# Scores of causal attention by 64 keys, with only the queries that may see them, and the first roots written to PSUM a step later

## Chip, cores and metric

The kernel runs on one core of a Trainium2 chip, all in fp32. The metric is device time in microseconds (us) of one execution, the median of the runs of a kernel. The core has five engines that run side by side and wait for each other by semaphores: TensorE (PE in the profile; its weight loads are shown apart as PEld), VectorE (DVE), ScalarE (ACT), GpSimd (POOL) and SyncE (SP), which issues the transfers. [...]

## What is computed

The input x has the shape (2, 256, 128, 128): batch, time, bands, channels. Three residual blocks follow each other; the first is causal attention over the 256 times of each of the 2x128 sequences, with four heads of 32 channels. The other two (attention over bands within 16 of each other, and a feed-forward block) are left out of this extract.

```python
def _mha(x, wi, bi, wo, bo, h, mask):
    qkv = x @ wi.T + bi
    q, k, v = jnp.split(qkv, 3, axis=-1)
    ...
    scores = jnp.einsum('...hqd,...hkd->...hqk', q, k) * (1.0 / np.sqrt(dh)) + mask
    attn = jax.nn.softmax(scores, axis=-1)
    o = jnp.einsum('...hqk,...hkd->...hqd', attn, v)
    o = o.swapaxes(-2, -3).reshape(x.shape)
    return o @ wo.T + bo
...
cm = _causal_mask(x.shape[1])
xt = _ln(x, ln_t_w, ln_t_b).transpose(0, 2, 1, 3)
x = x + _mha(xt, t_wi, t_bi, t_wo, t_bo, H_T, cm).transpose(0, 2, 1, 3)
```

## The kernel before

**Groups and steps.** The work is cut into groups of four tiles of 128 rows. A group of the time stage (class `OverTime`) is two sequences of 256 times, so each sequence is two tiles; there are 128 such groups. After them come the groups of the band attention (`OverBands`) and of the feed-forward block (`FeedForward`), in runs of eight. `run` (from L1029) goes through steps n and calls, by hand, the parts of several groups in each: every engine executes its instructions in exactly the order in which `run` calls them (`InOrder`), and the semaphore waits are put in by the framework from the tiles that instructions share. All instructions are recorded at one helper's line, L859, so a group of instructions is known by its tiles.

**A step of the time stage** calls, in this order: the scores (`time_scores`, L726: second key tile of group n, "old", and first key tile of group n+1, "new", interleaved in a fixed list of sixteen calls that ends with heads 1 and 2 of the second tile); the exponentials of the scores, six 128-partition instructions on ScalarE in a row (`second_weights` of heads 0 and 3, `first_weights` of heads 1 and 2, `second_weights` of heads 1 and 2); the mask of the second tile and `add(0)` on GpSimd; transfers; `statistics` of group n+5 on VectorE (four bn_stats and four bn_aggr); `normalize` and `turn` of group n+4 on VectorE (xh, and z, the 32x32 transpose, which four DMAs write to memory in a turned order, from where a later `fetch` reads xnT); `weigh` of group n-1 on TensorE (rp, the sums of the weights, and op, the weighted values); `invert` on ScalarE (ln and r, the reciprocals); the two remaining first exponentials, `mask_first` and `add(1)`; `output` of group n-2 on TensorE (yp) and `finish` on VectorE (res); `divide` of group n-1 on VectorE (rp, u, oT); queries and keys of group n+2 (qp, kp on TensorE, qT and kT on ScalarE); then the root of group n+5; `bias` on GpSimd; and the values (vp on TensorE, copied to v by ScalarE).

**The root.** `root_by_scalar` computes 1/sqrt(var + eps) roughly on ScalarE, as Exp(-0.5 Ln(var + eps)), for four columns; `refine` takes one Newton step on it with three VectorE instructions (`vy`, `vy`, `rstd`). `root0` is an SBUF tile. `normalize` of that group comes one step later.

**Scores.** A product of a head has the head's 32 channels as rows, 128 keys as the columns of the weights and the queries as the moving operand. The first key tile meets 256 queries and the second the 128 that come after it; the part above the diagonal is computed and then set to 0 by GpSimd's affine_select after the exponential. Each head has a bank of its own. TensorE works on the four heads' row groups side by side; the other products (`product`) are cut into four column groups of 32.

**Banks.** In the time stage each bank has a name, and the names turn round after each step:

```python
self.banks = dict(zip(("a1", "a2", "b0", "b3", "a0", "a3", "b1", "b2"), range(8)))
...
Attention.place = dict(rp=b["b0"], op=b["b3"], yp=b["a1"], qp=b["a2"], kp=b["b1"], vp=b["b2"])
...
self.banks = dict(
    a1=b["a1"], a2=b["a2"], b0=b["a0"], b3=b["a3"], a0=b["b0"], a3=b["b1"], b1=b["b3"], b2=b["b2"]
)
```

So `s1` of head 2 (the second tile's scores, 256 columns) and later in the step `vp` (512 columns) share bank b2; and the bank of `op`, which `divide` reads last, is the bank of head 1's second scores in the next step, that of `rp` the bank of head 0's first scores.

Of the kernel before, what the change touches and what calls it, by code (L numbers as in the profile page):

```python
# [10 lines left out]
F32 = mybir.dt.float32  # L11
# [9 lines left out]
H = 4  # L21
# [6 lines left out]
GB = 16  # L28
RUN = 32
SAFE = 30.0  # L30
LARGE = 1e20
EXP_SET = "natural_log_exp_and_others"

# [391 lines left out]
class Group:  # L425
# [30 lines left out]
        gpsimd.tensor_scalar(self.rstd, self.mv[:, :, 1], EPS, None, ALU.add)  # L456
        gpsimd.tensor_tensor(self.rstd, self.rstd, path.k.mhalf, ALU.pow)

    def root_by_scalar(self):

        path = self.path
        ln = path.small.tile([P, NT], F32, name="lnv")
        path.scalar.activation(ln, self.mv[:, :, 1], AF.Ln, bias=path.eps)
        self.root0 = path.small.tile([P, NT], F32, name="root0")
        path.scalar.activation(self.root0, ln, AF.Exp, scale=-0.5)

    def refine(self):

# [89 lines left out]

class Attention(Group):
    which = None  # L560
    place = {}

    def bias(self):
# [23 lines left out]
    def values(self):  # L587
        path = self.path
        wv = path.k.wf[self.which][:, 2 * P : 3 * P]
        self.vp = path.bank([P, NT, P], "vp", self.place.get("vp"))  # L590
        for i in range(NT):
            product(path, self.vp[:, i], self.xnT[:, i * P : (i + 1) * P], wv)

    def take_values(self):
        path = self.path
# [43 lines left out]
def rows_of(h):  # L639
    return slice(h * D, (h + 1) * D)  # L640


def product(path, out, weights, x, start=True, stop=True):


    for c in range(P // D):
        path.tensor.matmul(out[rows_of(c)], weights[:, rows_of(c)], x, start=start, stop=stop)


class OverTime(Attention):  # L650

    which = 0
    early, late = (1, 2), (0, 3)

    def first_tiles(self):
# [10 lines left out]

    def first_scores(self, h, s):
        r, a = rows_of(h), 2 * s * P  # L670
        self.path.tensor.matmul(
            self.s0[h][:, s], self.kT[r, a : a + P], self.qT[r, a : a + 2 * P], start=True, stop=True
        )

    def second_scores(self, h, s):
        r, a = rows_of(h), (2 * s + 1) * P
        self.path.tensor.matmul(
            self.s1[h][:, s], self.kT[r, a : a + P], self.qT[r, a : a + P], start=True, stop=True
        )

    def first_weights(self, heads):
        for h in heads:
# [3 lines left out]
        for h in heads:  # L686
            self.path.scalar.activation(self.p1[:, :, h, 0], self.s1[h], AF.Exp)

    def mask(self, blk):
        path = self.path  # L690
        path.gpsimd.affine_select(
            out=blk, in_=blk, compare_op=ALU.is_ge, fill=path.zero, base=0,
            pattern=[[0, 2], [0, H], [1, P]], channel_multiplier=-1,
        )

    def mask_first(self):
        self.mask(self.p0[:, :, :, 0:P])

    def mask_second(self):
        self.mask(self.p1[:, :, :, 0])  # L700

    def add(self, s):
        self.path.gpsimd.tensor_tensor(self.p1[:, s, :, 1], self.p1[:, s, :, 0], self.p0[:, s, :, P : 2 * P], ALU.add)
# [160 lines left out]
class BoundedPath:  # L864
    def __init__(self, ctx, tc, k):
        self.tc, self.nc, self.k = tc, tc.nc, k
        self.xpool = ctx.enter_context(tc.tile_pool(name="xpool", bufs=3))
        self.work = ctx.enter_context(tc.tile_pool(name="work", bufs=3))
        self.small = ctx.enter_context(tc.tile_pool(name="small", bufs=6))
        self.ps = ctx.enter_context(tc.tile_pool(name="ps", bufs=1, space=PSUM))  # L870
        self.next_bank = 0
        self.held = {}
        self.banks = dict(zip(("a1", "a2", "b0", "b3", "a0", "a3", "b1", "b2"), range(8)))
        self.tensor, self.vector = InOrder(tc, tc.nc.tensor), InOrder(tc, tc.nc.vector)
        self.scalar, self.gpsimd = InOrder(tc, tc.nc.scalar), InOrder(tc, tc.nc.gpsimd)
        self.sync = InOrder(tc, tc.nc.sync)
        self.dram = ctx.enter_context(tc.tile_pool(name="turns", bufs=3, space=DRAM))
        self.zero = 0.0
        self.once = once = ctx.enter_context(tc.tile_pool(name="once", bufs=1))
        self.eps = once.tile([P, 1], F32, name="eps")  # L880
        tc.nc.vector.memset(self.eps, EPS)

        self.band = once.tile([P, P], F32, name="band")
        tc.nc.gpsimd.memset(self.band, 0.0)
        for s in (1, -1):
            tc.nc.gpsimd.affine_select(
                out=self.band, in_=self.band, compare_op=ALU.is_ge, fill=-1e30, base=BAND,
                pattern=[[-s, P]], channel_multiplier=s,
            )
# [4 lines left out]

    def bank(self, shape, name, i=None):

        return self.ps.tile(shape, F32, name=name, tag=f"ps{self.turn_of_bank() if i is None else i}")

    @staticmethod
    def of_times(ap, i, f):  # L900
# [128 lines left out]
    def run(self, x, out):  # L1029
# [21 lines left out]
        for n in range(-12, len(groups) + 2):  # L1051
            feeds = [at(n - 2 + i, FeedForward) for i in range(5)]
            bands = [at(n - 2 + i, OverBands) for i in range(5)]
            turn = feeds[2] and bands[1]
            old, new = (groups[i] if at(i, OverTime) else None for i in (n, n + 1))
            if bands[2] and feeds[1]:
                self.scalar.preload_act_table_set(EXP_SET)
            do_at(n + 4, FeedForward, "root")
            do(n, "first_half", "first_function", "first_mask")
            if old is not None or new is not None:  # L1060
                time_scores(old, new)
                b = self.banks
                Attention.place = dict(rp=b["b0"], op=b["b3"], yp=b["a1"], qp=b["a2"], kp=b["b1"], vp=b["b2"])
            else:
                Attention.place = {}
            if old is not None:
                old.second_weights(old.late)
            if new is not None:
                new.first_weights(new.early)
            if old is not None:  # L1070
                old.second_weights(old.early)
                old.mask_second()
                old.add(0)
            if turn:
                do(n, "second_half", "second_function")
            do_at(n + 3, OverTime, "fetch")
            do_at(n + 2, (OverBands, FeedForward), "fetch")

            for i in (2 * n + 12, 2 * n + 13) if n < -2 else (n + 10,) if n < 2 else ():
                if i >= NT:  # L1080
                    do(i, "load")
            if n < -8 or n >= 0:
                do(n + 12, "load")
            if n >= 0:
                do_at(n + 5, OverTime, "statistics")
                for i in due[n]:
                    do(i, "statistics")
            do_at(n + 3, (OverBands, FeedForward), "normalize", "turn")
            do_at(n + 4, OverTime, "normalize", "turn")
            if n < 0:  # L1090
                do(n + 5, "statistics")
            do_at(n + 5, FeedForward, "statistics")
            if n == -4:
                self.fold_rest()
                self.warm()
            do(n - 1, "weigh")
            do(n - 1, "invert_exactly" if turn else "invert")
            if new is not None:
                new.first_weights(new.late)
                new.mask_first()  # L1100
            if old is not None:
                old.add(1)
            if bands[2] or turn or old is not None:
                do(n - 2, "output", "finish")
            do(n - 1, "divide")
            if not turn:
                do(n, "second_half", "second_function")
            if n in run0:
                do(n, "bias")
            if not bands[2] and old is None:  # L1110
                do_at(n, FeedForward, "bias")
                do_at(n + A, OverBands, "bias")
                if at(n - 1, FeedForward) and at(n - 2, OverBands):
                    do_at(n + A - 1, OverBands, "statistics", "root")
                if not turn:
                    do_at(n + A, OverBands, "statistics", "root")
            do_at(n + 2, OverTime, "queries_keys", "take_query", "take_key")
            do_at(n + 1, OverBands, "queries_keys", "take_query", "take_key")
            do_at(n + 5, OverTime, "root_by_scalar", "refine")
            for i in due[n]:  # L1120
                do(i, "root_by_scalar", "refine")
            do_at(n, OverTime, "bias")
            if not bands[2] and not turn and old is None:
                do(n - 2, "output", "finish")
            do_at(n + 2, OverTime, "values", "take_values")
            do_at(n + 1, OverBands, "values", "take_values")
            if old is not None or new is not None:

                b = self.banks
                self.banks = dict(  # L1130
                    a1=b["a1"], a2=b["a2"], b0=b["a0"], b3=b["a3"], a0=b["b0"], a3=b["b1"], b1=b["b3"], b2=b["b2"]
                )
# [69 lines left out]
```

## Time and profile before

| what | us |
|---|---|
| median of 3 runs | 2708.69 (2707.76 to 2710.78) |
| span of the profiled execution | 2709.9 |
| of it, up to the end of the time stage | about 957 |
| ACT, busy in the window 60 to 957 us | 789.56 |
| POOL, busy in the same window | 723.86 |

The groups of instructions in the window 100 to 900 us, which holds 110 steps of the time stage (columns: line, engine, operation, tiles, shapes, count, then busy us, mean ns of one, then idle us of the engine just before them and what ended it):

```profile
L859 PE MATMUL sp<-qT,kT 32*128 32x256 f32 x1758 | 174.2, 387 | 0.0
L859 PEld LDWEIGHTS sp<-qT,kT 32*128 32x128 f32 x3517 | 155.3, 185 | 23.0 <-ACT kT L859 21.8
L859 PE MATMUL sp<-qT,kT 32*128 32x128 f32 x1755 | 150.0, 286 | 0.0
L859 POOL TENSOR_SCALAR_AFFINE_SELECT p<-p 128x1024 f32<-128x1024 f32 x219 | 239.7, 1095 | 144.0 <-ACT p L859 144.0
L859 DVE SCALAR_TENSOR_TENSOR vy<-mv,root 128x4 f32<-128x4 f32 x110 | 115.7, 1052 | 0.0
L859 ACT ACTIVATE lnv<-mv,eps 128x4 f32<-128x4 f32 x110 | 32.9, 299 | 0.0
```

A shape such as 32*128 is the rows and columns of the weights that are in use; 32x256 is the moving operand. Matmuls overlap, so a group's busy time is less than its count times its mean. A step runs two of the GpSimd masks and one each of the last two rows. An engine's idle time matters only if what ended it lies on the chain of waits.

### The profile page before, as it was taken

The numbers are of one execution on the slowest core, as the hardware profiler recorded it, in microseconds if no ns is written. First come the engines' busy times: TensorE is split into PE (matmuls) and PEld (weight loads), VectorE is DVE, ScalarE is ACT, GpSimd is POOL, SyncE is SP. The second block draws the span as 40 slices with busy tenths as digits, with TensorE's granted clock in tenths as the row PEclk, the third lists the DMA queues.
The fourth block names the chain that finished last, engine by engine and source line by source line (L and its number), as shares of the span: only waits on it lengthen the run. The fifth ranks groups of instructions, "written<-read, shape, count | busy, mean of one in ns | idle before, by whom it ended". The sixth has DMA issues, their size and how long they took to land.

```text
span 2709.9 us, 139654 instructions
## 1 busy us (share of the span) xinstructions
PE 2677.1 (99%) x60470; PEld 1831.5 (68%) x60470; DVE 2279.5 (84%) x6708; ACT 1845.1 (68%) x3620; POOL 1864.3 (69%) x2169
## 2 busy tenths in 40 slices
PE   7999999999999999999999999999999999999998
PEld 5666676766676666666667766666666666666665
DVE  7999999999999997868769779688697796886874
ACT  5888888888888874655746646557456465565563
POOL 3788888878887876667657566666676666665762
PEclk9999999999999999999999999999999999999999
DMA  5555555555555535445444454444444444544533
GB/s 145 142 151 145 147 150 144 149 147 145 149 141 148 150 99 132 108 119 133 110 124 125 108 130 113 120 129 114 121 127 110 124 119 119 130 109 123 134 91 84
DMA packets 471442, 346.00 MB, mean 128 GB/s; under 512 B 43296, under 2 KB 405152, under 8 KB 470816
## 3 DMA queue, kind: packets, MB, share of 16 engines
q1 hardware_dynamic: 469568, 335.92, 47.8%
q8 instruction: 476, 7.80, 1.2%
q10 hardware_dynamic: 1248, 1.05, 0.2%
q14 instruction: 150, 1.23, 0.2%
HBM read 169.03 MB, written 167.77 MB: 124 GB/s over the span
## 4 chain that ended last, share of the span: by engine, by line
PE 84%; DVE 12%; DMA 2%; issue 1%; SPq 0%; ACT 0%; DVEq 0%; ACTq 0%
PE zp L859 17%; PE hp L859 14%; PE sp L859 11%; PE op L859 8%; PE rp L859 7%; PE vp L859 7%; PE qp L859 7%; PE kp L859 7%; PE yp L859 6%; DVE xh L859 2%; DVE stats L859 2%; DMA xnT<-turned 2%; DVE z L859 2%; DVE u L859 2%; DVE rp L859 1%; DVE x L859 1%
## 5 line engine op out<-in xcount | busy, mean ns | idle before, releaser
L859 ACT ACTIVATE hT<-hp,b 128x512 f32<-128x512 f32 x512 | 346.7, 687 | 533.3 <-PE hp L859 518.4
L859 POOL TENSOR_SCALAR_AFFINE_SELECT pf<-pf 128x512 f32<-128x512 f32 x768 | 476.9, 635 | 264.6 <-ACT pf L859 238.2
L859 DVE TENSOR_SCALAR xh<-x,mv,rstd 128x160 f32<-128x160 f32 x1536 | 597.5, 432 | 14.2
L859 PEld LDWEIGHTS zp<-w2T_sb,hT 128*32 128x32 f32 x16384 | 459.3, 110 | 61.5 <-issue 37.2
L859 PE MATMUL zp<-w2T_sb,hT 128*32 128x128 f32 x16384 | 475.8, 273 | 0.2 <-ACT hT L859 0.2
L859 PE MATMUL hp<-xnT,w1f 128*32 128x512 f32 x4096 | 474.6, 592 | 0.0
L859 ACT ACTIVATE p<-sp 128x512 f32<-128x512 f32 (+1 forms) x1024 | 417.1, 500 | 15.7 <-PE sp L859 4.0
L859 POOL TENSOR_SCALAR_AFFINE_SELECT p<-p 128x1024 f32<-128x1024 f32 x256 | 280.2, 1094 | 190.8 <-ACT p L859 190.8
L859 PE MATMUL sp<-qT,kT 32*128 32x128 f32 (+1 forms) x8192 | 361.2, 310 | 3.2 <-DVE oT L859 1.8
L859 PEld LDWEIGHTS sp<-qT,kT 32*128 32x128 f32 x8192 | 309.2, 185 | 56.9 <-ACT kT L859 48.0
L859 PEld LDWEIGHTS vp<-wf,xnT 128*32 128x32 f32 x8192 | 232.7, 110 | 157.3 <-issue 138.8
L859 POOL TENSOR_TENSOR p<-p,p 128x512 f32<-128x512 f32 x256 | 328.8, 1284 | 10.7
L859 DVE BATCH_NORM_STATS2 stats<-x 128x6 f32<-128x128 f32 x1536 | 327.1, 276 | 1.0 <-DMA x<-in_x 1.0
L859 ACT ACTIVATE pf<-sp 128x512 f32<-128x512 f32 x512 | 264.7, 603 | 60.4 <-PE sp L859 59.6
L859 PEld LDWEIGHTS hp<-xnT,w1f 128*32 128x32 f32 x4096 | 156.3, 110 | 190.0 <-issue 115.5
L859 DVE STREAM_TRANSPOSE z<-xh 128x512 f32<-128x512 f32 x384 | 273.3, 712 | 13.2
L859 DVE TENSOR_TENSOR res<-zp,res 128x512 f32<-128x512 f32 x128 | 87.6, 684 | 223.5 <-PE zp L859 223.5
L859 PE MATMUL yp<-wn,oT 128*32 128x128 f32 x8192 | 271.8, 273 | 0.0
L859 PE MATMUL vp<-wf,xnT 128*32 128x128 f32 x8192 | 270.9, 273 | 0.0
L859 POOL TENSOR_TENSOR rstd<-rstd,mhalf 128x4 f32<-128x4 f32 x248 | 256.6, 1035 | 20.7
L859 PE MATMUL qp<-xnT,wf 128*32 128x512 f32 x2048 | 267.2, 592 | 2.0 <-ACT p L859 2.0
L859 ACT ACTIVATE qT<-qp,bq 128x512 f32<-128x512 f32 x256 | 176.1, 688 | 134.4 <-PE qp L859 134.3
(92 smaller groups left out, 4003.1 us busy)
## 6 DMA issues: line engine op xcount, KB each, us to landing
turned<-z SPq DMA_DIRECT2D x1536, 64.0 KB, 2.2
xnT<-turned SPq DMA_DIRECT2D x384, 256.0 KB, 3.1
x<-in_x SPq DMA_DIRECT2D x128, 256.0 KB, 4.2
x<-res SPq DMA_DIRECT2D x256, 128.0 KB, 2.4
x<-x SPq DMA_DIRECT2D x128, 256.0 KB, 4.4
out<-res SPq DMA_DIRECT2D x256, 128.0 KB, 2.5
w1T_sb<-in_w1T ACTq DMA_DIRECT2D x1, 256.0 KB, 6.8
w2T_sb<-in_w2T ACTq DMA_DIRECT2D x1, 256.0 KB, 8.3
```

The source lines that it names most:

```text
L859: return self.tc.keep_in_program_order(emit(*args, **kwargs))
```

## The change

- **Scores.** A product is cut into two of 64 keys. The first key tile's upper half (keys 64 to 127) gets only the queries from 64 on; of the second tile the upper half (keys 64 to 127, with the queries from 64 on) is written to partitions 0 to 63 and the lower half (all 128 queries) to partitions 64 to 127. The columns left out are not written: what the bank held before goes through the exponential there, and the mask sets it to 0.
- **Values.** In tiles 1 and 3 (the second key tile of each sequence) `product` takes the weight columns, which are the keys, in the order 2, 3, 0, 1 (its `turn` is added to c, modulo four), so that the rows of v stand as those of the scores do.
- **Mask of the second tile.** Two affine_selects, one on partitions 0 to 63 over 128 queries, one on partitions 64 to 127 over the first 64.
- **Roots.** Groups of the time stage write `root0` to the last four columns of bank b2, in the step after; the two ScalarE instructions stand ahead of the step's exponentials, the three of `refine` between `statistics` and `normalize`. The groups of the bands keep `root_by_scalar` with an SBUF tile.
- **Banks.** Each bank is one tile for the whole run, of which `bank` returns a part, in place of a new tile at each use.

```diff
-    def root_by_scalar(self):
+    def root_by_scalar(self, to=None):
...
-        self.root0 = path.small.tile([P, NT], F32, name="root0")
+        self.root0 = path.small.tile([P, NT], F32, name="root0") if to is None else to
         path.scalar.activation(self.root0, ln, AF.Exp, scale=-0.5)
+
+    def root_in_bank(self):
+        path = self.path
+        self.root_by_scalar(path.ps[path.banks["b2"]][:, BANK - NT :])
...
-            product(path, self.vp[:, i], self.xnT[:, i * P : (i + 1) * P], wv)
+            product(path, self.vp[:, i], self.xnT[:, i * P : (i + 1) * P], wv, turn=2 if i in self.swapped else 0)
...
+    swapped = (1, 3)
...
     def first_scores(self, h, s):
         r, a = rows_of(h), 2 * s * P
-        self.path.tensor.matmul(
-            self.s0[h][:, s], self.kT[r, a : a + P], self.qT[r, a : a + 2 * P], start=True, stop=True
-        )
+        for e in range(0, P, HALF):
+            self.path.tensor.matmul(
+                self.s0[h][e : e + HALF, s, e:], self.kT[r, a + e : a + e + HALF], self.qT[r, a + e : a + 2 * P],
+                start=True, stop=True,
+            )
 
     def second_scores(self, h, s):
         r, a = rows_of(h), (2 * s + 1) * P
-        self.path.tensor.matmul(
-            self.s1[h][:, s], self.kT[r, a : a + P], self.qT[r, a : a + P], start=True, stop=True
-        )
+        for e in range(0, P, HALF):
+            q = P - HALF - e
+            self.path.tensor.matmul(
+                self.s1[h][e : e + HALF, s, q:], self.kT[r, a + q : a + q + HALF], self.qT[r, a + q : a + P],
+                start=True, stop=True,
+            )
...
     def mask_second(self):
-        self.mask(self.p1[:, :, :, 0])
+        self.mask(self.p1[0:HALF, :, :, 0], -HALF)
+        self.mask(self.p1[HALF:P, :, :, 0, 0:HALF])
...
-        self.ps = ctx.enter_context(tc.tile_pool(name="ps", bufs=1, space=PSUM))
+        ps = ctx.enter_context(tc.tile_pool(name="ps", bufs=1, space=PSUM))
+        self.ps = [ps.tile([P, BANK], F32, name=f"bank{i}", tag=f"bank{i}") for i in range(8)]
...
+            do_at(n + 4, OverTime, "root_in_bank")
             if old is not None:
                 old.second_weights(old.late)
...
-            do_at(n + 4, OverTime, "normalize", "turn")
+            do_at(n + 4, OverTime, "refine", "normalize", "turn")
...
-            do_at(n + 5, OverTime, "root_by_scalar", "refine")
```

More of the change, by code (lines that the diff above doesn't have):

```diff
@@ L30 @@
 SAFE = 30.0
+BANK = 512
+HALF = P // 2
 LARGE = 1e20
@@ L560 @@
     which = None
+    swapped = ()
     place = {}
@@ L640, in rows_of, with product @@
     return slice(h * D, (h + 1) * D)
-def product(path, out, weights, x, start=True, stop=True):
+def product(path, out, weights, x, start=True, stop=True, turn=0):
     for c in range(P // D):
-        path.tensor.matmul(out[rows_of(c)], weights[:, rows_of(c)], x, start=start, stop=stop)
+        path.tensor.matmul(out[rows_of(c)], weights[:, rows_of((c + turn) % NT)], x, start=start, stop=stop)
 class OverTime(Attention):
     which = 0
+    swapped = (1, 3)
     early, late = (1, 2), (0, 3)
@@ L687, in second_weights, with mask @@
             self.path.scalar.activation(self.p1[:, :, h, 0], self.s1[h], AF.Exp)
-    def mask(self, blk):
+    def mask(self, blk, base=0):
         path = self.path
         path.gpsimd.affine_select(
-            out=blk, in_=blk, compare_op=ALU.is_ge, fill=path.zero, base=0,
-            pattern=[[0, 2], [0, H], [1, P]], channel_multiplier=-1,
+            out=blk, in_=blk, compare_op=ALU.is_ge, fill=path.zero, base=base,
+            pattern=[[0, 2], [0, H], [1, blk.shape[-1]]], channel_multiplier=-1,
         )
@@ L895, in bank @@
     def bank(self, shape, name, i=None):
-        return self.ps.tile(shape, F32, name=name, tag=f"ps{self.turn_of_bank() if i is None else i}")
+        flat = self.ps[self.turn_of_bank() if i is None else i][:, 0 : math.prod(shape[1:])]
+        if len(shape) == 2:
+            return flat
+        names = "abc"[: len(shape) - 1]
+        sizes = dict(zip(names, shape[1:]))
+        return flat.rearrange(f"p ({' '.join(names)}) -> p {' '.join(names)}", **sizes)
     @staticmethod
```

## The prediction

> **What bounds the kernel now.** I read the page first. Its line of busy times says that TensorE hardly rests; the chain of waits puts the time stage, the only one that the change touches, at 32 to 957 us.
>
> ```profile
> PE 2677.1 (99%) x60470; PEld 1831.5 (68%) x60470; DVE 2279.5 (84%) x6708; ACT 1845.1 (68%) x3620; POOL 1864.3 (69%) x2169
> ```
>
> Then the stage by itself, in the view of windows (columns: stretch, length, busy PE, PEld, DVE, ACT, POOL, clock, DMA share, GB/s). PE is busy all of the time, but VectorE 97% of it: two engines share the lead.
>
> ```profile
> 100.00:900.00 800.00, 800.00 (x17513) 557.53 (x17507) 777.33 (x2186) 703.88 (x1642) 646.89 (x549) 1.00 0.56 147
> ```
>
> Third, the chain of waits cut to one step (start, length, what). A step is scores, sums, weighted values, output, queries, keys, values: 401.90 to 409.19 is 7.29 us, and the mean over the stage is 7.31 (every third step is some 0.06 longer). PE's own order is the whole chain.
>
> ```profile
> 401.90 1.53 PE sp L859 x24
> 403.42 1.00 PE rp L859 x16
> 404.42 1.30 PE op L859 x32
> 405.72 0.87 PE yp L859 x32
> 406.60 0.86 PE qp L859 x8
> 407.46 0.86 PE kp L859 x8
> 408.31 0.87 PE vp L859 x32
> 409.19 1.56 PE sp L859 x25
> ```
>
> Last, the timeline of the engines that feed it. The reader is to see that VectorE's oT ends at 402.65, inside PE's scores, and that the first refine line lasts 1.07 us for four columns, while GpSimd's bias runs to 403.63.
>
> ```profile
> 401.96 0.69 DVE L859 TENSOR_TENSOR oT<-op,u 128x512 f32<-128x512 f32 x1
> 402.57 1.07 DVE L859 SCALAR_TENSOR_TENSOR vy<-mv,root 128x4 f32<-128x4 f32 x1
> 403.68 0.16 DVE L859 SCALAR_TENSOR_TENSOR vy<-vy,root 128x4 f32<-128x4 f32 x1
> 403.88 0.16 DVE L859 SCALAR_TENSOR_TENSOR rstd<-vy,root 128x4 f32<-128x4 f32 x1
> 405.02 1.58 DVE L859 TENSOR_SCALAR xh<-x,mv,rstd 128x160 f32<-128x160 f32 x4
> 409.29 0.69 DVE L859 TENSOR_TENSOR oT<-op,u 128x512 f32<-128x512 f32 x1
> ```
>
> ```profile
> 401.90 0.20 ACT L859 ACTIVATE root<-lnv 128x4 f32<-128x4 f32 x1
> 402.01 0.57 ACT L859 COPY v<-vp 128x512 f32<-128x512 f32 x1
> 402.68 2.19 ACT L859 ACTIVATE p<-sp 128x256 f32<-128x256 f32 x6
> ```
>
> [...] vy with mv and root takes 1.07 us and ends with GpSimd's bias, the next two take 0.16. [...] The trace shows it only for four tiles (128x32: 32 of vp in 0.87 us, eight in a row per column group, 0.109 each).
>
> **Part 1, scores by 64 keys.** A head's scores are two instructions per product, and 128 columns of one take 0.109 us. Before, a head's row group streams 2x256 and 2x128 columns, twice: 1536 columns, 1.31 of the 1.53 us. After, each half of the row group streams 2x(256+64) or 2x(192+128) = 640, twice: 1.09 us, if the halves run side by side. That is 0.22 less; the first weight load is shorter too (185 ns for 128 columns, 110 for 32, so about 135 for 64): 0.05. Together 0.27 us a step. The other bound: halves one after the other, 2560 columns, 2.18 us, 0.87 more. I take side by side, as the column groups of vp do.
>
> **Part 2, halves exchanged.** The values' weight columns only change places: nothing. GpSimd's second mask becomes two: the 64-partition one keeps its 1024 elements per partition (1.09 us), the other has 512 (0.63 in the bands' row pf). GpSimd goes from 6.0 busy us a step to 6.6, and its chain from the last exponential to add(1) grows by 0.6.
>
> **Part 3, the roots.** Ln and Exp move, on ScalarE, from ahead of the copy of v to ahead of the six exponentials of the next step; no DMA moves, and none waits for them. The three refine instructions move on VectorE from the step's end past four statistics and four aggregates to just before normalize. [...]
>
> But the roots lie in bank b2, which also holds head 2's second scores, the last product of the scores. [...] ScalarE's Exp must wait for the end of all scores, and the six exponentials are queued behind it. VectorE's refine must wait until the exponential of head 2, the last of the six, has read the bank; behind it are queued xh, z, res, rp, u and oT; SP's four DMAs of z and the stores and the fetch behind them come later too, but what they fetch is multiplied two steps on. And PE's head-1 scores go into the bank that oT reads: they wait for oT, and head 2's follow them. That closes a ring within one step:
>
> - oT's end to the end of the last score: before, 402.65 to 403.42 (TensorE's timeline has the last twelve of sp from 402.80 for 0.62) is 0.77; 0.72 with the shorter load
> - PE's end to ScalarE: qp ends at 407.46, qT starts at 407.52: 0.06
> - Exp to the next ScalarE instruction, as 401.90 to 402.01: 0.11
> - six exponentials: 2.19
> - ScalarE to the waiting engine: 404.87 to GpSimd's mask at 404.94: 0.07
> - refine: three times 0.20 (403.68 to 403.88)[...]: 0.79
> - xh to the end of oT: 405.02 to 409.98: 4.96
>
> Sum 8.90 us a step, against 7.31: 1.59 more. Parts 1 and 2 vanish in it: PE needs 7.04, GpSimd 6.6. The ring holds in the steps that have both old scores in b2 and a group of the time stage to refine, 124 of the 128: +197 us. Against the profile's own 2709.9 us this is 2907; the runs' median lies 1.2 lower, so 2906. The bounds of the terms: last scores 0.55 to 1.1 (the upper if PE is slow after its pauses: at the stage's end, after 3 us without work, the chain has rp at 1.86 where it is 1.00), refine 0.5 to 1.0, the rest of VectorE 4.8 to 5.2; 8.4 to 9.4 us a step, 2845 to 2970.
>
> ```profile
> 963.98 0.70 DVE u L859
> 964.68 0.02 issue
> 964.71 0.70 DVE oT L859
> 965.41 0.14 issue
> 965.54 1.03 PE sp L859 x8
> 966.57 1.86 PE rp L859 x16
> ```
>
> These lines, the chain at the end of the time stage, show the link oT to scores when VectorE is late.
>
> **Rivals.**
> - *Writes are ordered by bank, reads are not.* Then refine waits only for Exp. Scores end 1.31 us after their start (1.60 now), exponentials start at 1.48 in place of 0.85, end at 3.67; GpSimd follows with mask 1.09, 0.57, a gap of 0.08, add 1.25, mask 1.06, add 1.28 to 9.1. The second half of rp needs it in the next step, 5.3 us before the one after that: (9.1+5.3)/2 = 7.2 us a step, GpSimd now the bound, 2709.9-127x0.08 = 2699. Faster by 0.4%. For it: nothing in the trace speaks against two readers. [...]
> - *Waits by bytes only.* No wait at all, PE bound with GpSimd near it: 7.1 us, 2683. [...]
> - *The Exp's wait is hidden, only the reads are ordered.* From oT 0.72, the last two exponentials 0.7, 0.07, 0.79, 4.96, 0.06: 7.3 us, no change, 2709.
> - *The halves do not overlap, and the reads are not ordered:* PE 7.31+0.87 = 8.18, 2820, slower by another way. With the ring, only its last scores are longer (0.2), inside the range.
> - *The other side* of my forecast is the first rival; it decides if refine starts less than 2 us after the scores' end.
>
> **How the numbers follow.** Ring 0.78 (2845 to 2970 holds nine tenths of that), reads unordered 0.09, bytes only 0.04, hidden 0.04, no overlap 0.05. I widen the low end to 2800, to take in the last: 0.70+0.05 and some tails of the ring, 0.8. A change under 0.2% can't be told from none by a measurement of this kernel. Slower: ring and no overlap, 0.83, and a small part of the first rival, 0.84; same: hidden and a part of the first, 0.06; faster 0.10.
>
> **What would show it.** Right: scores 8.9 us apart; VectorE idle some 2 us ahead of vy, released by ScalarE's p; ScalarE idle ahead of root, released by PE sp; PE idle within sp, released by VectorE; vy near 0.2 us; two masks where there was one; the stages after 957 us as long as before. Wrong: scores 7.0 to 7.3 us apart and vy right behind the aggregates (reads unordered), or sp over 2 us of unbroken work (no overlap).

## The result, and the profile after

The changed kernel takes 2885.93 us, the median of 4 runs (2885.28 to 2889.16); the kernel before, on the same chip, 2709.74. The ratio is 1.0652, with a 95% interval of 1.0639 to 1.0664. The profiled execution spans 2887.4 us, 177.5 more than that of before. The last copy of kT of the time stage begins at 1133.2 us where it began at 957.0: 176.1 of the 177.5 us are lost inside the time stage, and what follows takes 1754.2 us (1752.8 before). A step takes 8.73 us in place of 7.31. All tiles that lie in PSUM, eight of 128 partitions by 512 fp32 columns, are now named `bank` (line L873), so groups are told apart by their other operands.

The page's line of busy times: TensorE has fallen from 99% to 95% of a longer span.

```profile
PE 2745.4 (95%) x64566; PEld 1835.9 (64%) x64566; DVE 2190.6 (76%) x6708; ACT 1844.7 (64%) x3620; POOL 1949.9 (68%) x2297
```

The same stretch of the time stage in the view of windows (columns as before: stretch, length, busy PE, PEld, DVE, ACT, POOL, clock, DMA share, GB/s):

```profile
100.00:900.00 800.00, 719.88 (x17600) 475.92 (x17600) 585.22 (x1830) 590.16 (x1376) 600.03 (x550) 1.00 0.47 124
```

PE was busy for 800 of these 800 us and is now idle for 80. No other engine comes near 800: the stage has no busiest engine that bounds it any more, which is what a ring of waits looks like. The clock is 1.00 in both, and the transfers only thin out with the longer step.

The chain of waits over one step (start, length, what) hands from engine to engine where it was PE alone:

```profile
412.47 1.43 PE bank L873 x29
...
413.98 0.18 ACT bank L873
414.16 2.11 ACT p L873 x6
...
416.29 0.17 DVE vy L873
...
416.67 0.17 DVE rstd L873
...
416.87 1.15 DVE xh L873 x3
...
419.15 0.65 DVE res L873
419.80 0.62 DVE bank L873
```

Here "PE bank" are the scores, "ACT bank" is the Exp that writes the root to PSUM, and "DVE bank" is rp. So: scores, Exp, six exponentials, refine, xh, z, res, rp, then u, which follows rp on VectorE, and scores again. The other step in the same view is followed back over PE's products instead (405.79, 4.14 us), with 0.50 us without a cause ahead of res; VectorE's timeline has no idle time between vy and oT, so the ring is the same. The view of waits says the same for 100 to 900 us (waiting group, what released it: idle us, count, longest):

```profile
DVE vy L873 <- ACT p L873: 192.5, 92, 2.4
POOL p L873 <- ACT p L873: 186.5, 92, 2.3
ACT bank L873 <- PE bank L873: 137.6, 91, 1.8
PEld bank L873 <- ACT p L873: 109.7, 184, 1.2
PE bank L873 <- ACT p L873: 60.0, 92, 0.9
```

The first and the third are the two waits that the root in bank b2 brings: 92 and 91 of them, one each per step, 192.5/92 = 2.1 and 137.6/91 = 1.5 us long. The fifth, PE's products behind ScalarE's p, was not foreseen (see e7). The timelines of VectorE, ScalarE and TensorE (start, length, instruction, in brackets the idle time before it and its releaser) give every term of the ring (some lines between are left out):

```profile
403.73 0.69 DVE L873 TENSOR_TENSOR oT<-bank,u 128x512 f32<-128x512 f32 x1
404.34 0.86 DVE L873 BATCH_NORM_STATS2 stats<-x 128x6 f32<-128x128 f32 x4
405.12 0.36 DVE L873 BATCH_NORM_AGGREGATE mv<-stats 128x2 f32<-128x6 f32 x4
407.57 0.16 DVE L873 SCALAR_TENSOR_TENSOR vy<-mv,bank 128x4 f32<-128x4 f32 x1 [2.09 <-ACT p L873]
...
407.95 0.16 DVE L873 SCALAR_TENSOR_TENSOR rstd<-vy,bank 128x4 f32<-128x4 f32 x1
408.15 1.61 DVE L873 TENSOR_SCALAR xh<-x,mv,rstd 128x160 f32<-128x160 f32 x4
412.45 0.69 DVE L873 TENSOR_TENSOR oT<-bank,u 128x512 f32<-128x512 f32 x1
```

```profile
403.45 0.30 ACT L873 ACTIVATE lnv<-mv,eps 128x4 f32<-128x4 f32 x1
405.26 0.18 ACT L873 ACTIVATE bank<-lnv 128x4 f32<-128x4 f32 x1 [1.51 <-PE bank L873]
405.37 2.16 ACT L873 ACTIVATE p<-bank 128x256 f32<-128x256 f32 x6
```

```profile
402.83 0.69 PE L873 MATMUL bank<-qT,kT 32*64 32x64 f32 x24
403.75 1.39 PE L873 MATMUL bank<-qT,kT 32*64 32x256 f32 x40 [0.23 <-DVE u L873]
405.79 1.07 PE L873 MATMUL bank<-p,ones 128*32 128x256 f32 x16 [0.65 <-ACT p L873]
```

The reader is to see that `vy` sits idle for 2.09 us behind the aggregates, although the root that it reads was written at 405.44: what it waits for is the last of the six exponentials, which reads other columns of the same bank. And ScalarE is idle for 1.51 us ahead of an Exp whose input, from the Ln right before it, is ready: it waits for the last scores, which are written to other columns of that bank.

### The profile page after: what moved, and what is told of

Read it like the earlier page. It is cut to its first block, busy times and chain, and to the rows that moved or that the text cites. A ratio compares the mean times of both kernels' runs of the same rounds, so it can differ in the third digit from the quotient of the medians.

```text
span 2887.4 us, 148446 instructions
## 1 busy us (share of the span) xinstructions
PE 2745.4 (95%) x64566; PEld 1835.9 (64%) x64566; DVE 2190.6 (76%) x6708; ACT 1844.7 (64%) x3620; POOL 1949.9 (68%) x2297
## 3 DMA queue, kind: packets, MB, share of 16 engines
q8 instruction: 508, 8.32, 1.3%
q14 instruction: 154, 1.26, 0.2%
## 4 chain that ended last, share of the span: by engine, by line
PE 56%; DVE 29%; ACT 8%; issue 4%; DMA 1%; SPq 0%; ACTq 0%; POOL 0%; DVEq 0%
PE bank L873 56%; DVE xh L873 8%; ACT p L873 7%; DVE bank L873 5%; DVE u L873 5%; DVE res L873 3%; DVE z L873 2%; DVE stats L873 2%; DVE x L873 1%; DVE vy L873 1%; DMA xnT<-turned 1%; ACT bank L873 1%; DVE mv L873 1%; DVE rstd L873 1%; DVE oT L873 1%
## 5 line engine op out<-in xcount | busy, mean ns | idle before, releaser
L873 ACT ACTIVATE hT<-bank,b 128x512 f32<-128x512 f32 x512 | 347.0, 688 | 532.9 <-PE bank L873 515.4
L873 POOL TENSOR_SCALAR_AFFINE_SELECT pf<-pf 128x512 f32<-128x512 f32 x768 | 478.7, 638 | 263.2 <-ACT pf L873 236.8
L873 DVE TENSOR_SCALAR xh<-x,mv,rstd 128x160 f32<-128x160 f32 x1536 | 600.8, 433 | 18.8
L873 POOL TENSOR_SCALAR_AFFINE_SELECT p<-p 128x1024 f32<-128x1024 f32 (+2 forms) x384 | 364.6, 950 | 285.2 <-ACT p L873 276.7
L873 PEld LDWEIGHTS bank<-w2T_sb,hT 128*32 128x32 f32 x16384 | 457.1, 110 | 63.7 <-issue 39.7
L873 PE MATMUL bank<-xnT,wf 128*32 128x512 f32 x4096 | 488.2, 594 | 4.7 <-ACT p L873 4.7
L873 PE MATMUL bank<-w2T_sb,hT 128*32 128x128 f32 x16384 | 474.3, 273 | 0.2 <-ACT hT L873 0.2
L873 PE MATMUL bank<-xnT,w1f 128*32 128x512 f32 x4096 | 472.7, 592 | 0.0
L873 PE MATMUL bank<-qT,kT 32*128 32x128 f32 (+4 forms) x12288 | 418.4, 301 | 30.8 <-DVE u L873 27.8
L873 ACT ACTIVATE p<-bank 128x512 f32<-128x512 f32 (+1 forms) x1024 | 413.7, 493 | 3.9 <-PE bank L873 3.5
L873 PEld LDWEIGHTS bank<-qT,kT 32*64 32x64 f32 (+1 forms) x12288 | 320.2, 149 | 124.4 <-DVE u L873 57.2
L873 DVE TENSOR_TENSOR res<-bank,res 128x512 f32<-128x512 f32 x256 | 171.1, 668 | 229.5 <-PE bank L873 228.8
L873 POOL TENSOR_TENSOR p<-p,p 128x512 f32<-128x512 f32 x256 | 328.2, 1282 | 10.7
L873 PEld LDWEIGHTS bank<-wf,xnT 128*32 128x32 f32 x8192 | 233.0, 110 | 158.4 <-issue 138.6
L873 DVE BATCH_NORM_STATS2 stats<-x 128x6 f32<-128x128 f32 x1536 | 326.4, 275 | 0.1
L873 ACT ACTIVATE pf<-bank 128x512 f32<-128x512 f32 x512 | 264.8, 602 | 60.7 <-PE bank L873 60.0
L873 DVE STREAM_TRANSPOSE z<-xh 128x512 f32<-128x512 f32 x384 | 273.4, 712 | 13.5
L873 PEld LDWEIGHTS bank<-xnT,w1f 128*32 128x32 f32 x4096 | 150.5, 110 | 193.9 <-issue 169.3
L873 PE MATMUL bank<-wn,oT 128*32 128x128 f32 x8192 | 271.9, 273 | 0.0
L873 PE MATMUL bank<-wf,xnT 128*32 128x128 f32 x8192 | 271.2, 273 | 0.1
L873 POOL TENSOR_TENSOR rstd<-rstd,mhalf 128x4 f32<-128x4 f32 x248 | 257.0, 1036 | 20.7
L873 POOL TENSOR_SCALAR rstd<-mv 128x4 f32<-128x4 f32 x248 | 56.8, 229 | 303.9 <-DVE mv L873 303.1
```

The costliest lines, as they stand in the source:

```text
L873: return self.tc.keep_in_program_order(emit(*args, **kwargs))
```

## The experiments

Each diff is against the changed kernel. The kernel before was run beside each of the three sets: 2710.48 us (e1 to e4), 2710.65 (e5 to e8) and 2710.83 (e9 to e11). e7 and e8 are medians of two runs, the others of four or more.

**e1: the root goes to SBUF, at the change's place.**

```diff
     def root_in_bank(self):
         path = self.path
-        self.root_by_scalar(path.ps[path.banks["b2"]][:, BANK - NT :])
+        self.root_by_scalar()
```

> The changed kernel with root0 in an SBUF tile again, written and refined at the changed places. Ring theory (the shared bank b2 makes Exp wait for the scores and refine for the exponentials): both waits go, scores 7.0 to 7.2 us apart, TensorE or GpSimd the bound, 2675 to 2695 us. Rival, the cost lies in the scores by 64 keys, their halves or the second mask: nothing changes, 2880 to 2890 us. Rival, the new places alone cost (Exp ahead of the six exponentials, refine behind the statistics): 2710 to 2800 us.

2718.56 us, ratio 1.0028 (1.0019 to 1.0038), 7.35 us a step. One argument of one instruction takes away 167 of the 176 us: the bank, not the place of the root and not the scores, is the cause. But 2675 to 2695 was expected, and it isn't there. TensorE's timeline shows why:

```profile
403.83 1.66 PE L873 MATMUL bank<-qT,kT 32*64 32x64 f32 x64
405.41 1.07 PE L873 MATMUL bank<-p,ones 128*32 128x256 f32 x16
```

From the start of the scores to the start of rp is 405.41-403.83 = 1.58 us, where before it was 1.53 and 1.26 had been forecast. PE is busy all the time again (800.00 of the 800 us), so these 0.05 us are paid in each step.

**e2: the roots alone**, with before's scores and one mask.

```diff
-    swapped = (1, 3)
+    swapped = ()
...
-        for e in range(0, P, HALF):
...
+        self.path.tensor.matmul(
+            self.s0[h][:, s], self.kT[r, a : a + P], self.qT[r, a : a + 2 * P], start=True, stop=True
+        )
...
-        self.mask(self.p1[0:HALF, :, :, 0], -HALF)
-        self.mask(self.p1[HALF:P, :, :, 0, 0:HALF])
+        self.mask(self.p1[:, :, :, 0])
```

> The changed roots and banks with the scores, the values and the one mask of the kernel before. Ring theory: the whole loss stays, and the last scores are a little longer: 8.7 to 8.9 us a step, 2885 to 2905 us. Rival, the scores by 64 keys cost: 2700 to 2715 us.

2893.49 us, 1.0676 (1.066 to 1.0692), 8.77 us a step: the roots carry the whole loss. In the ring the scores by 64 keys are worth 0.04 us a step.

**e3: the scores alone**, with the root as before the change (SBUF, at the end of the step).

```diff
-            do_at(n + 4, OverTime, "root_in_bank")
...
-            do_at(n + 4, OverTime, "refine", "normalize", "turn")
+            do_at(n + 4, OverTime, "normalize", "turn")
...
+            do_at(n + 5, OverTime, "root_by_scalar", "refine")
```

> The scores by 64 keys, with exchanged halves and two masks, and the roots where the kernel before has them, in SBUF. Ring theory: no ring; TensorE needs 7.04 us a step, but VectorE has no gap in the 7.31 us[...], so 7.0 to 7.25 us, 2670 to 2703 us. Rival, the halves of a row group run one after the other: 8.1 us or more, over 2800 us. Rival, GpSimd's second mask is the bound: 7.3 us or more, 2705 to 2730 us.

2730.87 us, 1.0078 (1.0064 to 1.0092): slower by itself, against 2670 to 2703 expected. Besides the longer section, VectorE is late. GpSimd's bias and VectorE's second `vy`:

```profile
401.84 1.28 POOL L873 TENSOR_TENSOR res<-x,orow 128x512 f32<-128x512 f32 x1
```

```profile
401.94 1.20 DVE L873 SCALAR_TENSOR_TENSOR vy<-vy,root 128x4 f32<-128x4 f32 x1
```

The second `vy` takes 1.17 to 1.20 us and ends, as the first did before the change, with GpSimd's bias; but the bias now stands behind one more mask and ends 2.43 us after the start of the scores (403.12 against 400.69) in place of 1.80 (403.63 against 401.83). So oT ends at 409.28 in a section that runs from 408.13 to 409.93, heads 1 and 2 have to wait for it, and the section takes 1.67 to 1.80 us. The time lies just above the range of the rival, a bound by GpSimd's second mask (2705 to 2730); but GpSimd is busy for only 702 of the 800 us, so it delays by its order and not as the bound. What the masks alone cost was not measured.

**e4: the root in b2, but behind the six exponentials.**

```diff
-            do_at(n + 4, OverTime, "root_in_bank")
             if old is not None:
                 old.second_weights(old.late)
...
                 old.second_weights(old.early)
+            do_at(n + 4, OverTime, "root_in_bank")
+            if old is not None:
                 old.mask_second()
```

> The changed kernel with Ln and Exp of the root behind the six exponentials in place of ahead of them; bank b2 as in the change. Ring theory: Exp and refine still wait for bank b2, but four of the six exponentials no longer wait for the end of the scores. From u's end: scores 1.49, two exponentials 0.6, Ln and Exp 0.5, refine 0.6, xh to u 4.3, together 7.4 to 7.5 us a step, 2720 to 2740 us. Rival, sharing the bank costs by itself whatever the order: 2860 to 2890 us.

2763.99 us, 1.02 (1.0185 to 1.0216), 7.73 us a step. The exponentials no longer stand behind the Exp, and two thirds of the loss go. More was expected to go. The sum made beforehand ran through one step; the ring that is there runs through two. Timelines of VectorE and TensorE:

```profile
401.82 0.16 DVE L873 SCALAR_TENSOR_TENSOR vy<-mv,bank 128x4 f32<-128x4 f32 x1 [1.09 <-ACT bank L873]
...
405.98 0.69 DVE L873 SCALAR_TENSOR_TENSOR u<-bank,r 128x512 f32<-128x512 f32 x1
```

```profile
398.35 2.05 PE L873 MATMUL bank<-qT,kT 32*64 32x64 f32 x64
...
406.09 2.03 PE L873 MATMUL bank<-qT,kT 32*64 32x64 f32 x64
408.05 1.07 PE L873 MATMUL bank<-p,ones 128*32 128x256 f32 x16
...
413.81 1.53 PE L873 MATMUL bank<-qT,kT 32*64 32x64 f32 x44
```

Scores begin at 398.35; six exponentials, Exp, refine and VectorE's row end with u at 406.67, 8.32 later. That is after the next scores have begun, so these wait within themselves, and rp starts 1.38 after u. From there PE's own order takes 5.76 to the scores after next. (8.32+1.38+5.76)/2 = 7.73, the measured step. The three pieces fill two steps without a gap, so the sum has to come out; what it shows is which waits and which orders the two steps consist of.

**e5: root in SBUF, the scores' halves issued in another order.** e1's edit and:

```diff
-    def first_scores(self, h, s):
+    def first_scores(self, h, s, es):
...
-        for e in range(0, P, HALF):
+        for e in es:
...
+    both = (0, HALF)
+    for heads, second, s, es in (
+        ((0,), 1, 0, both), ((1, 2), 0, 0, both), ((3,), 1, 0, both), ((0, 3), 1, 1, (0,)), ((0, 3), 1, 1, (HALF,)),
+        ((0, 3), 0, 0, (0,)), ((1, 2), 0, 1, (HALF,)), ((1, 2), 0, 1, (0,)), ((0, 3), 0, 0, (HALF,)),
+        ((0, 3), 0, 1, (0,)), ((0, 3), 0, 1, (HALF,)), ((1, 2), 1, 0, (HALF,)), ((1, 2), 1, 0, (0,)),
+        ((1, 2), 1, 1, (HALF,)), ((1, 2), 1, 1, (0,)),
+    ):
```

> The root in SBUF as in e1_root_in_sbuf, and the products of the scores issued half by half in the order in which their part of the array comes free. Theory of the queue (the halves do overlap, but one half of head 1 or 2 is held back behind instructions whose part is busy, so the section takes 1.58 us in place of 1.26): 1.2 to 1.35 us of scores, 7.0 to 7.15 us a step, 2675 to 2697 us, faster than the kernel before. Rival, each of the 64 instructions costs a fixed time, so that order is without effect: 7.35 us a step, 2712 to 2722 us.

2710.06 us, 1.0001 (0.9992 to 1.0009). The order alone gives back 8.5 us against e1; 2697 or less was expected, and it isn't there. VectorE, whose first `vy` still takes 0.84 to 0.95 us (401.80 and 416.31), is now nearly as late as PE; e9, where that line takes 0.12 us, shows that this costs little: 7.24 us a step in place of 7.29.

**e6: e1 and e2 together**: the change's places and its one tile per bank, root in SBUF, scores by 128 keys.

> Scores by 128 keys, the root in SBUF, written and refined at the changed places, the banks as whole tiles. Theory: places and bank tiles alone cost nothing while TensorE is the bound: 7.31 us a step, 2705 to 2713 us. Rival, the new places cost by themselves: 2720 us or more, as e1_root_in_sbuf already hints with 2718.

2707.34 us, 0.999 (0.9981 to 0.9998). The new places and the bank tiles cost nothing.

**e7: only the Exp's wait.** Exp to b2 stays, but refine reads a second Exp in SBUF.

```diff
-        self.root_by_scalar(path.ps[path.banks["b2"]][:, BANK - NT :])
+        ln = path.small.tile([P, NT], F32, name="lnv")
+        path.scalar.activation(ln, self.mv[:, :, 1], AF.Ln, bias=path.eps)
+        path.scalar.activation(path.ps[path.banks["b2"]][:, BANK - NT :], ln, AF.Exp, scale=-0.5)
+        self.root0 = path.small.tile([P, NT], F32, name="root0")
+        path.scalar.activation(self.root0, ln, AF.Exp, scale=-0.5)
```

> The changed kernel with one Exp more: Exp still writes b2 ahead of the six exponentials, so it waits for the scores, but refine reads a second root in SBUF, so it doesn't wait for the exponentials. If both waits together close the ring, this one alone costs little: exponentials 0.9 us later than in e1_root_in_sbuf, GpSimd's chain to the sums then sets some 7.5 us a step, 2725 to 2755 us. Rival, this wait alone is the loss: 2870 us or more.

2820.81 us, 1.0407 (1.0388 to 1.0426), 8.15 us a step, well above the 2755 expected. This run found the link that the prediction had missed. TensorE's timeline:

```profile
400.28 1.07 PE L877 MATMUL bank<-p,ones 128*32 128x256 f32 x16 [0.72 <-ACT p L877]
...
406.05 1.66 PE L877 MATMUL bank<-qT,kT 32*64 32x64 f32 x64
408.42 1.07 PE L877 MATMUL bank<-p,ones 128*32 128x256 f32 x16 [0.72 <-ACT p L877]
```

The sums rp are written to bank b0, which holds head 0's second scores, and so wait for their exponential. That one stands right behind the Exp, which waits for the last score. (The second Exp, which this run adds between them, holds it up by another 0.10 us, 407.91 to 408.01 on ScalarE.) PE is otherwise unbroken: rp to vp 406.05-400.28 = 5.77, scores 1.66, wait 0.72, together 8.15. What looked like a wait on an engine with slack is a wait on PE, because PE's next instruction needs the first thing queued behind it.

**e8: only a read of b2 ahead of refine.** Root in SBUF, and a copy of four columns of b2 on VectorE, to bring the reads' wait alone.

```diff
+            if old is not None:
+                self.vector.tensor_copy(self.small.tile([P, NT], F32, name="seen"), self.ps[self.banks["b2"]][:, 0:NT])
             do_at(n + 4, OverTime, "refine", "normalize", "turn")
```

> The kernel e1_root_in_sbuf with one VectorE copy of four columns of b2 ahead of refine: refine waits until head 2's exponential has read b2, Exp waits for nothing. Ring over two steps as in e4_root_after_six: 7.6 to 7.8 us a step, 2745 to 2775 us. Rival, this wait alone is the loss: 2870 us or more.

2877.68 us, 1.0617 (1.0597 to 1.0636), 8.67 us a step, but it doesn't measure what it was made for. VectorE in it:

```profile
408.74 0.16 DVE L873 COPY seen<-bank 128x4 f32<-128x4 f32 x1 [0.70 <-ACT p L873]
408.82 1.07 DVE L873 SCALAR_TENSOR_TENSOR vy<-mv,root 128x4 f32<-128x4 f32 x1
...
410.12 0.50 DVE L873 SCALAR_TENSOR_TENSOR rstd<-vy,root 128x4 f32<-128x4 f32 x1
410.65 1.61 DVE L873 TENSOR_SCALAR xh<-x,mv,rstd 128x160 f32<-128x160 f32 x4
```

The last exponential releases both the copy and GpSimd's two masks, which run from 408.78 for 1.83 us. So refine, now with its root in SBUF, meets the masks head on and takes 1.83 us (408.82 to 410.65) where the changed kernel has 0.58. An estimate without that: 8.67-1.25 = 7.42 us a step, near the 7.35 that PE's own order takes in e1, if nothing else holds the step back. What the reads' wait costs when nothing else is added was not measured; the run does show what the root in PSUM spares, 1.25 us in this place.

**e9, e10, e11: a later place for the root.** In all three the root stays in b2, but Exp and refine are called behind `turn`, for the group after. On ScalarE that puts Ln and Exp right behind the six exponentials, as in e4; on VectorE it puts refine behind xh and z in place of ahead of them. e10 is this alone, e9 has e5's order of the halves too, e11 has scores by 128 keys.

```diff
-            do_at(n + 4, OverTime, "root_in_bank")
...
-            do_at(n + 4, OverTime, "refine", "normalize", "turn")
+            do_at(n + 4, OverTime, "normalize", "turn")
             if n < 0:
                 do(n + 5, "statistics")
+            do_at(n + 5, OverTime, "root_in_bank", "refine")
```

> The scores of e5_halves_in_order, and the root in bank b2 with another place: Ln and Exp behind the six exponentials, for the group whose statistics were just taken, and refine behind z, ahead of res. Then Exp and refine find the bank read and free, nothing that the scores need stands behind them for long[...]. Theory, that the first experiments were held at 7.3 us[...] (oT late, so heads 1 and 2 late): TensorE the bound at 7.0 to 7.1 us, 2672 to 2690 us, faster than both. Rival, that the 64-key products themselves cost 7.3 us: 2700 to 2715 us.

> The changed kernel with that other place of the root alone, the scores in the order of the change. If VectorE's lateness held e1_root_in_sbuf at 7.35 us: 7.0 to 7.15 us a step, 2675 to 2695 us. If the order of the products did (halves held back in TensorE's queue): 7.25 us or more, 2700 to 2715 us.

> The other place of the root with the scores by 128 keys of the kernel before, as a control. TensorE stays the bound with 1.53 us of scores: 7.29 us a step, 2702 to 2712 us, whatever VectorE gains. Rival, that the place of the root alone brings a gain: under 2695 us.

| kernel | us | ratio (95%) | step, us | scores to rp, us |
|---|---|---|---|---|
| e9, halves reordered | 2707.6 | 0.9988 (0.9982 to 0.9995) | 7.24 | 1.47 |
| e10, change's order | 2721.4 | 1.0039 (1.0025 to 1.0052) | 7.35 | 1.58 |
| e11, 128 keys | 2711.19 | 1.0002 (0.9994 to 1.001) | 7.29 | 1.52 |

All three are free of the ring, with the root in the same bank. ScalarE and VectorE in e10:

```profile
400.31 2.19 ACT L873 ACTIVATE p<-bank 128x256 f32<-128x256 f32 x6
...
402.70 0.18 ACT L873 ACTIVATE bank<-lnv 128x4 f32<-128x4 f32 x1
```

```profile
403.03 0.12 DVE L873 SCALAR_TENSOR_TENSOR vy<-mv,bank 128x4 f32<-128x4 f32 x1
...
404.41 0.69 DVE L873 TENSOR_TENSOR res<-bank,res 128x512 f32<-128x512 f32 x1 [0.88 <-POOL p L873]
```

The bank is used again at once: Exp follows the six exponentials by 0.2 us and `vy` follows Exp by 0.15. Nobody stands idle for it, because VectorE has xh and z to do until then. Later in the step it is idle for 0.87 us in the mean, ahead of res, yet the kernel is slower than before: the section of scores decides, and it follows the order in which the halves are issued. The rest of PE's order is the same 5.77 us in e10 (7.35-1.58) and in e9 (7.24-1.47). So the 2672 to 2690 us expected of e9 are not there either: its section is only 0.06 us shorter than the 1.53 of before. TensorE's timelines of e10 and then of e9, from which the last column comes:

```profile
399.44 1.66 PE L873 MATMUL bank<-qT,kT 32*64 32x64 f32 x64
401.03 1.07 PE L873 MATMUL bank<-p,ones 128*32 128x256 f32 x16
```

```profile
401.50 1.55 PE L877 MATMUL bank<-qT,kT 32*64 32x64 f32 x64
402.97 1.07 PE L877 MATMUL bank<-p,ones 128*32 128x256 f32 x16
```

Do the halves run side by side at all? The section says so by itself: it is shorter than the 2.18 us that a row group's 2560 columns would need with its halves one after the other, estimated from the 0.109 us that 128 columns take in vp. How well they are filled is less plain. From the recorded ends of the single matmuls one can work out how many of the eight parts of the array (four row groups by two halves) stream at once: each is taken to stream for 0.85 ns per column (vp's 0.109 us for 128), up to 0.16 us before its recorded end (0.273-0.109 in the row of zp). Matmul ends are modelled, so this is an estimate, as a mean over the steps of 100 to 900 us, with the first column as the start:

```
us from start     0.05  0.30  0.50  0.65  0.80  1.05  1.10  1.15  1.20  1.25
e10               7.8   7.8   7.0   6.2   8.0   7.7   5.0   2.3   1.5   1.0
e9                7.8   8.0   7.0   5.7   8.0   7.9   5.5   3.0   1.6   1.0
```

By this estimate eight parts stream at once for most of the section. Time is lost in a dip in the middle and in a tail, in which one or two parts work alone after the others have run out: until 1.45 in e10, until 1.33 in e9. In the kernel before, by the same estimate, all four parts run until 1.30 and stop nearly together. So the 0.27 us were not lost to halves that exclude each other but, by the estimate, to parts that stand empty in the middle and at the end. Why they do is open; that the order of issue moves the section by 0.11 us (1.58 to 1.47) is shown.

No version beats the kernel before by more than the 0.2% that can be told from none: e6 and e9 stand 0.1% under it.

## Why the prediction was right, point by point

**Slower, by a ring through bank b2: right, and shown.** Taking the bank away (e1), or moving Exp past the exponentials of that bank and refine past xh and z (e10, e11), takes the loss away; the roots alone (e2) bring it. The waits show at the places named: VectorE idle 2.1 us ahead of vy by ScalarE's p, ScalarE idle 1.5 us ahead of the root by PE, PE idle 0.23 us within the scores by VectorE (403.75). Waits stand between accesses to different columns: of a write behind writes (Exp behind the scores) and of a read behind reads (`vy` behind the exponentials). The program sets them. That it would set them by bank, for reads too, the forecast had assumed, and the trace of before held no such pair; what would happen on the chip without them was not tried.

**The terms**, at 403 to 414 us, each between the same ends as in the forecast:

| term | predicted | measured |
|---|---|---|
| oT's end to last score, and to ScalarE | 0.72+0.06 | 0.84 (404.42 to 405.26) |
| Exp to the next ScalarE instruction | 0.11 | 0.11 |
| six exponentials | 2.19 | 2.16 |
| ScalarE to refine | 0.07 | 0.04 (407.53 to 407.57) |
| refine | 0.79 | 0.58 (407.57 to 408.15) |
| xh to the end of oT | 4.96 | 4.99 (408.15 to 413.14) |
| sum | 8.90 | 8.72 |

The mis-sized term is refine, 0.21 us too long; the others together are 0.03 too short. The first link is drawn a little differently in the trace: what releases PE is u (it ends at 403.70, and head 0's scores go into the bank of rp, which u reads), ahead of oT at 404.42, which heads 1 and 2 still need. The trace has the forecast's link too: weight loads of the scores that carry a wait for VectorE start at 404.47, 0.05 us after oT's end. Which of the two decides wasn't separated; both lie on the same row of VectorE. Of the 0.79, three times 0.20 comes from the trace of before; the rest, an allowance for a source in PSUM, was shown by no trace. The runs show no such addition: with a source in PSUM the three take 0.158 us each and start 0.19 apart (407.57, 407.76, 407.95); with all in SBUF the second and third of before take 0.163 and start 0.20 apart. Over 124 steps 0.18 us is 22 us, about the 20 between 2906 and 2886. The upper bound's slow PE after its pauses did not come: the clock is 1.00, and rp takes 1.07 us after a wait of 0.65, as in e1 without one.

**The scores' 0.27 us: wrong.** It made no difference to the forecast, since the ring covered it, and that is luck: the step is false by itself, 1.58 us and not 1.26 (e1, e10). It assumed that eight parts that run side by side stay filled; the column groups of vp, from which that was taken, have eight equal products each in a row, the scores have unequal ones in an order that is tied to the banks. That this is the reason was not shown.

**The masks: right.** GpSimd has 600.03/91.7 = 6.5 us a step (91.7 steps of 8.73 in 800 us), 0.6 more than before; the second mask takes 0.66 (0.63 forecast), and it lies beside the ring. e3 shows what it costs where VectorE waits for what comes after it on GpSimd.

**`vy` near 0.2 us: right.** The first line goes from 1.07 us to 0.16, and the freed time lies ahead of it, as idle time. With mv and root in SBUF it ended in the kernel before at 403.64, with GpSimd's bias (403.63), and in e8 the three lines ended at 410.62, with GpSimd's masks (410.61); with the root in PSUM the second and third take 0.16 us each while GpSimd's masks run (407.61 to 409.42). What holds the one up and not the other was not shown beyond these times.

**The rivals.** None happened as such, and two were priced wrongly. *Writes ordered, reads not*, the other side, was put at 2699: e7 makes nearly this case (refine waits for an Exp alone) and takes 2820.81. Its sum sent the late exponentials to GpSimd and overlooked that PE's rp waits for the first of them, by bank b0; with 8.15 us a step, some 0.10 of it from the added Exp, it is slower too. So the direction did not hang on the order of reads, as the forecast had it: the Exp's wait alone is enough, and the order of reads adds the rest, 8.73-8.15 = 0.58 or, without the added Exp, an estimated 0.68. *The Exp's wait hidden*, put at 7.3 us, is near to e4, and there a ring over two steps makes 7.73. *No overlap* would have given a section of 1.53+0.87 = 2.40 us; it takes 1.58. *Bytes only* is refuted by the two waits.

The rest of the kernel was forecast unchanged and is.

## What to carry to other kernels

As the waits of these runs show (2.1 us a step ahead of `vy`, 1.5 ahead of Exp), a few columns of a PSUM bank are not free for other data just because nobody writes them: whoever reads or writes them is queued with everything that uses the bank, and with everything behind him in his own engine's order. Before data is put into a shared bank, write down who touches the bank last before and first after, on every engine, and add up the ring. Then look, in each engine's order, for a place right behind the bank's previous user where the engine has other work until the bank is free: here Exp behind the six exponentials and refine behind z, two calls moved past `turn`, took 2886 down to 2721 with the bank the same. And a product cut into more parts should be priced by how long its last part works and not by its columns alone: here 1.09 us by columns became a section of 1.47 to 1.58, where 1.31 had made 1.53 before.

## What was not expected of the hardware

- Four columns from PSUM cost VectorE no more than from SBUF: 158 ns in the changed kernel against 163 in the kernel before, for the second and third scalar_tensor_tensor of `refine`. ScalarE's Exp of four columns takes 177 ns to PSUM (changed kernel) and 206 to SBUF (before; 0.19 us right behind another Exp, in e7).
- GpSimd's mask costs the same on half the partitions: 64x1024 takes 1090 ns in the changed kernel, 128x1024 took 1095 before; 64x512 takes 660 ns, where the bands' mask of 128x512 took 635 before.
- With products by 64 keys, the same multiplications in another order took 1.47 (e9) in place of 1.58 us (e10).
